# Moving layernorm centring and two time-step operations from VectorE to ScalarE, and folding a router constant into its matmul

## The chip, the cores and the metric

The kernel runs on one core of one Trainium2 chip. The core has a tensor engine (TensorE, PE in the profile) for matmuls and transposes, VectorE (DVE), ScalarE (ACT), GpSimd (POOL) and the queue that issues transfers (SyncE, SP). Each engine carries out its own instructions strictly in order; an instruction that has to wait for another engine holds up all that stands behind it in its queue. The metric is the device time of one execution in microseconds. Three runs of the kernel before took 2607.37, 2610.11 and 2611.04, a median of 2610.11.

## The reference

The input x has 4 sequences of 256 tokens with 512 features, all float32. Four pre-layernorm blocks are applied one after the other:

```
x = x + attention(layernorm(x))      # block 1: gated linear attention, 32 heads of 128
x = x + router(layernorm(x))         # block 2
x = x + state_space(layernorm(x))    # block 3: 128 heads of 64, 8 groups
x = x + adapters(layernorm(x))       # block 4: 64 adapters of rank 16, the 16 best per token

layernorm(x) = (x - mean) / sqrt(var + 1e-5)          # over the 512 features

router(n):   scores  = softmax(n @ Wr.T + b)          # 64 experts
             w       = scores, where among the token's 8 largest, else 0
             out     = n * sum(w) + w @ expert_bias

time steps of blocks 1 and 3:  dt = softplus(n @ Win.T + dt_bias)
```

In block 3 and in block 1 the time steps scale the values and give decays by a cumulative sum along the tokens. Block 4 takes for each token a softmax over its 16 largest router scores and multiplies the 64x16 hidden values by these gates before the second matrix.

## The kernel before, in words

x is held on the chip as 8 tiles k.x[0] to k.x[7] of 128 tokens by 512 features. Tiles 0 to 3 are half 0, tiles 4 to 7 half 1, and each block is run half by half, so that half 1 of one block runs beside half 0 of the next. For the matmuls with weights, the normalized x is turned (features on the partitions) and split into two fp32r parts, xs_hi and xs_lo, and so are the weights: the high part is a cast on ACT (L138), the low part a subtraction on POOL (L141). A projection (proj, L193) is three matmuls for each of four feature chunks. Weights come in 512 KB pieces into a small number of raw buffers (raw_wx, raw_wo, raw_wa, raw_wb and so on); a piece's transfer can start when the piece before it in its buffer has been split.

Layernorm: moments (L82) takes bn_stats (L86) and bn_aggr (L88) on DVE and rstd = (var + eps)^-0.5 on POOL (L90 and L91). centre (L95) makes xn = (x - mean) * rstd in one DVE operation (L99) over 128x512, 32 of them in the kernel. turned (L103) transposes xn in four pieces on PE (L107). In blocks 1, 3 and 4, normalize (L111) then takes xs_hi with ACT (L124) and xs_lo with DVE (L125), and centres a later tile; xn has one buffer there. In block 2 the router's own loop does the same with xT (ACT, L604) and the score matmul (ps_lg, L596).

Time steps: steps_of (L206) projects to ps_dt, adds the bias with DVE into vT (L216), transposes it (L220), copies it to dt with DVE (L221), and goes on with the softplus by DVE and ACT in turn, a cumulative sum on PE and a transfer of the sum (cum), which comes back spread over the partitions (gb). There are four: each half of blocks 1 and 3.

Router: router (L574) has a route generator for each half. After softmax and top 8, the four tiles' weights are transposed (ps_t, L627) and copied by ACT to wT (L629, 64x512). For each tile POOL makes gain = 1 + sum(w)*rstd and a constant sum(w)*rstd*mean (L634 to L636), DVE computes x = x*gain - constant (L638), PE wT by expert_bias (o2, L642), and DVE adds that to x (L643).

State space: state_space (L649) has for each of 8 groups and each half the convolution (conv, L702, ACT L707 and three DVE operations L709), decay matrices m (L748; products with cb on DVE, exponentials on ACT), a mixer (L789: ps_y, xs, yh on ACT L813, yl on DVE L814) and an output matmul (ps_o, L849) that is added up in acc (L853 on ACT, L855 on DVE). At the end of a half x is updated by acc times r (L858), where r is a power on POOL (L835).

Adapters: adapters (L934) projects the normalized x to the router scores (ps_lg), takes the 16 largest (L971 to L991), turns the gates (gT, L996), writes them out and reads them back spread over partitions (gate, L1042), and multiplies the hidden values by them (L1051). wb is the second matrix, split as others by ACT (L1023) and POOL (L1024).

The order of the work is set on two levels. Lists written by hand (STEP1, SIDE1, STEP3, SIDE3) say which piece of a block follows which, and generators of the neighbouring block are pumped in between. On top of this the tile framework schedules with a simulated timeline, TileContext with schedule_with_timeline_sim=True, which fixes the order on every engine's queue when the kernel is built. So an edit of one operation can put many others in another order.

Of the kernel before, what the change touches and what calls it, by code (L numbers as in the profile page):

```python
# [11 lines left out]
F32 = mybir.dt.float32  # L12
# [6 lines left out]
P = 128  # L19
# [62 lines left out]
def moments(k, tc, t, tag):  # L82

    nc = tc.nc
    stats = k.small([P, 6], f"stats_{tag}_{t}", "ln_stats")
    nc.vector.bn_stats(stats, k.x[t])  # L86
    mv = k.small([P, 2], f"mv_{tag}_{t}", "ln_mv", 6)
    nc.vector.bn_aggr(mv, stats)  # L88
    rstd = k.small([P, 1], f"rstd_{tag}_{t}", "ln_rstd", 6)
    nc.gpsimd.tensor_scalar_add(rstd, mv[:, 1:2], EPS)  # L90
    nc.gpsimd.tensor_tensor(rstd, rstd, k.neghalf[:, 0:1], ALU.pow)  # L91
    return mv[:, 0:1], rstd


def centre(k, tc, t, of, tag, into="xn"):  # L95

    bufs = 1 if into == "xn" else 2
    xn = k.wk.tile([P, HID], F32, tag=into, name=f"xn_{tag}_{t}", bufs=bufs)
    tc.nc.vector.tensor_scalar(xn, k.x[t], *of, ALU.subtract, ALU.mult)  # L99
    return xn  # L100


# [103 lines left out]
def steps_of(k, tc, half, w, n, bias, amp, top, dt, start, cum, tag, spare, weigh=False, into="xn"):  # L206

    nc = tc.nc
    ps = proj(k, tc, w, half, f"dt{tag}_{half}", k.bank)
    room = k.wk.tile([P, FREE], F32, tag=into, name=f"room{tag}_{half}", bufs=1 if into == "xn" else 2)
    vT = room[0:n, :]
    nc.vector.tensor_scalar_add(vT, ps[0:n, :], bias)  # L216
    yield
    ps = k.psum.tile([P, HT, n], F32, tag=k.bank, name=f"ps_v{tag}_{half}")
    for t in range(HT):
        nc.tensor.transpose(ps[:, t, :], vT[:, t * P:t * P + P], k.ident[0:n, 0:n])  # L220
    nc.vector.tensor_copy(dt, ps.rearrange("p (b z) h -> p b z h", b=2))  # L221
    yield True


    spare = k.wk.tile([P, FREE], F32, tag=spare, name=f"e{tag}_{half}", bufs=4)
    e = spare[:, 0:HT * n].rearrange("p (b z h) -> p b z h", b=2, z=2)
    u = room[:, 0:HT * n].rearrange("p (b z h) -> p b z h", b=2, z=2)
    d = start.rearrange("p k h b -> p (k h b)")[:, 0:HT * n].rearrange(
        "p (b z h) -> p b z h", b=2, z=2
    )  # L230
    nc.vector.scalar_tensor_tensor(e, dt, -1.0, dt, ALU.mult, ALU.max)
    k.act(e, e, AF.Exp, scale=-1.0)
    nc.vector.tensor_scalar_add(u, e, 1.0)
    yield True
    k.act(d, u, AF.Ln)
    nc.vector.scalar_tensor_tensor(e, u, -1.0, e, ALU.add, ALU.subtract)
    nc.vector.scalar_tensor_tensor(d, u, -1.0, d, ALU.add, ALU.min)
    k.act(u, d, AF.Exp, scale=-1.0)
    nc.vector.scalar_tensor_tensor(dt, dt, 0.0, d, ALU.max, ALU.add)
    nc.vector.tensor_tensor(e, e, u, ALU.mult)  # L240
    nc.vector.tensor_tensor(dt, dt, e, ALU.subtract)
    if top is not None:
        nc.vector.tensor_scalar(dt, dt, 0.0, top, ALU.max, ALU.min)
    al = spare[:, 0:HT * n].rearrange("p (t h) -> p t h", t=HT)
    nc.vector.tensor_tensor(al, dt.rearrange("p b z h -> p (b z) h"), mid(amp, HT), ALU.mult)
    yield
    ps = k.psum.tile([n, HT, P], F32, tag=k.bank, name=f"ps_cum{tag}_{half}")
    for t in range(HT):
        nc.tensor.matmul(ps[:, t, :], al[:, t, :], k.upper, start=True, stop=True)
    cumT = room[0:n, :]  # L250
    nc.scalar.copy(cumT, ps.rearrange("h t l -> h (t l)"))
    for z in range(2):
        nc.sync.dma_start(
            cum[z].rearrange("h (b l) -> h b l", b=2),
            cumT.rearrange("h (b z l) -> h z b l", b=2, z=2)[:, z],
        )
    ps = k.psum.tile([P, 2, 2, n], F32, tag=k.bank, name=f"ps_in{tag}_{half}")
    nc.tensor.matmul(
        ps.rearrange("p b z h -> p (b z h)"), k.upper, spare[:, 0:HT * n],
        start=True, stop=True,  # L260
    )
    within = start[:, 0:2].rearrange("p z h b -> p b z h")
    across = start[:, 2].rearrange("p h b -> p b h")
    nc.vector.tensor_scalar_mul(within, ps, -1.0)
    yield True
    ps = k.psum.tile([P, 2, n], F32, tag=k.bank, name=f"ps_tail{tag}_{half}")
    nc.tensor.matmul(ps, k.lower, al[:, 0::2, :], start=True, stop=True)
    if weigh:

        nc.vector.tensor_scalar_max(e, dt, 1.2e-38)  # L270
        k.act(e, e, AF.Ln)
        nc.vector.tensor_tensor(across, ps, e[:, :, 0, :], ALU.add)
        nc.vector.tensor_tensor(within, within, e, ALU.add)
    else:
        k.act(across, ps, AF.Exp)
        nc.vector.tensor_tensor(across, across, dt[:, :, 0, :], ALU.mult)
    yield
# [296 lines left out]
def router(k, tc, io):  # L574
# [4 lines left out]
    nc.sync.dma_start(wr, io["L0_ffn_router_weight"])  # L579
    bias = k.room[:, 5 * SEQ - NE:5 * SEQ]  # L580
    nc.sync.dma_start(bias, io["L0_ffn_router_bias"].partition_broadcast(P))
    eb = k.room[0:NE, 6 * SEQ:8 * SEQ]
    nc.sync.dma_start(eb, io["L0_ffn_expert_bias"])

    def route(half):

        tiles = [HT * half + at for at in range(HT)]
        of = [moments(k, tc, t, "2") for t in tiles]
        lg = k.small([P, HT, NE], f"lg2_{half}", "lg", 1)
        xn = centre(k, tc, tiles[0], of[0], "2")  # L590
        yield
        for at in range(HT + 1):
            if at:
                ps = k.psum.tile([P, NE], F32, tag=k.bank, name=f"ps_lg2_{tiles[at - 1]}")
                for c in range(KC):
                    nc.tensor.matmul(  # L596
                        ps, xT[:, c, :], wr[:, c, :],
                        start=(c == 0), stop=(c == KC - 1),
                    )
                nc.vector.tensor_tensor(lg[:, at - 1, :], ps, bias, ALU.add)  # L600
            if at < HT:
                tag, bufs = ("y", 4) if half else ("xd", 2)
                xT = k.wk.tile([P, KC, P], F32, tag=tag, name=f"xT_{tiles[at]}", bufs=bufs)
                nc.scalar.copy(xT, turned(k, tc, xn, f"xn_2_{tiles[at]}"))  # L604
            if at + 1 < HT:
                xn = centre(k, tc, tiles[at + 1], of[at + 1], "2")
            yield at == HT
        sm = k.small([P, 2, HT], f"sm2_{half}", "sm")
        nc.vector.reduce_max(sm[:, 0, :], lg, axis=AX.X)
        nc.vector.tensor_tensor(lg, lg, last(sm[:, 0, :], NE), ALU.subtract)  # L610
        k.act(lg, lg, AF.Exp)
        yield
        nc.vector.reduce_sum(sm[:, 0, :], lg, axis=AX.X)
        nc.vector.reciprocal(sm[:, 0, :], sm[:, 0, :])
        nc.vector.tensor_tensor(lg, lg, last(sm[:, 0, :], NE), ALU.mult)

        top = k.small([P, HT, 16], f"top2_{half}", "top", 1)[:, :, 0:8]
        rest = k.small([P, HT, NE], f"rest2_{half}", "rest", 1)
        for at in range(HT):
            nc.vector.max(top[:, at, :], lg[:, at, :])  # L620
            nc.vector.match_replace(rest[:, at, :], top[:, at, :], lg[:, at, :], -1.0)
        nc.vector.scalar_tensor_tensor(lg, rest, 0.0, lg, ALU.is_lt, ALU.mult)
        nc.vector.reduce_sum(sm[:, 1, :], top, axis=AX.X)
        yield
        ps = k.psum.tile([NE, HT, P], F32, tag=k.bank, name=f"ps_t2_{half}")
        for at in range(HT):
            nc.tensor.transpose(ps[:, at, :], lg[:, at, :], k.ident)  # L627
        wT = k.wk.tile([P, HT, P], F32, tag="xd", name=f"wT2_{half}")[0:NE]
        nc.scalar.copy(wT, ps)  # L629
        yield  # L630

        by = k.small([P, 2, HT], f"by2_{half}", "sm")
        for at, (mean, rstd) in enumerate(of):
            nc.gpsimd.tensor_tensor(by[:, 0, at:at + 1], sm[:, 1, at:at + 1], rstd, ALU.mult)  # L634
            nc.gpsimd.tensor_tensor(by[:, 1, at:at + 1], by[:, 0, at:at + 1], mean, ALU.mult)
        nc.gpsimd.tensor_scalar_add(by[:, 0, :], by[:, 0, :], 1.0)  # L636
        for at, t in enumerate(tiles):
            nc.vector.tensor_scalar(  # L638
                k.x[t], k.x[t], by[:, 0, at:at + 1], by[:, 1, at:at + 1], ALU.mult, ALU.subtract
            )  # L640
            ps = k.psum.tile([P, HID], F32, tag=k.bank, name=f"ps_o2_{t}")
            nc.tensor.matmul(ps, wT[:, at, :], eb, start=True, stop=True)  # L642
            nc.vector.tensor_add(k.x[t], k.x[t], ps)  # L643
            yield

    return route
# [596 lines left out]
```

## Time and profile before

| | |
|---|---|
| median of three runs | 2610.11 us |
| the profiled execution's own time | 2612.82 us |
| its span in the profile | 2611.1 us |
| mean granted clock of TensorE in it | 0.978 of full speed |
| DVE centring L99, 32 times | 25.5 us busy, 547 ns median, 2182 ns the longest |
| ACT activations of 128x512 | 583 to 724 ns mean, by their operands |
| DVE L638, 8 times | 5.6 us busy, 541 ns median |

The profile is of one execution. A group of instructions is given by line, engine and operation with its count, its busy time and the mean duration of one. The chain of work that ended last is followed back from the last instruction, at each step to what released it. A time is counted from the start of the span. "xn<-x,mv,rstd" means that xn is written from x, mv and rstd. The granted clock (PEclk) tells at which share of its full speed TensorE was run in a stretch.

In the span, block 1 lasts to about 955 us, with half 0 of blocks 2 and 3 beside its end from about 690; half 1 of block 2 and the first part of block 3 follow until about 1070; block 3 goes on to about 2480, and block 4 stands at the end.

### The profile page before, as it was taken

Reading aid. Unit: us, or ns where it says so; the run is one execution under the profiler, and the core shown is the slowest. Engines: PE = TensorE matmul, PEld = TensorE weight load, DVE = VectorE, ACT = ScalarE, POOL = GpSimd, SP = SyncE. Lnnn points to the kernel's source line nnn. Section 1 sums busy time; section 2 is a strip of 40 time slices with the busy share of each in tenths; the row PEclk is TensorE's granted clock in tenths of the full one; section 3 lists DMA queues with packets and bytes.
Section 4 is the critical chain, followed back from the end, with each engine's and each line's share of the span. In section 5 each row is a group of like instructions: output and inputs, shape, how many; then the busy total and the mean of one; then the engine's idle time right before and its main releaser. Section 6 shows DMA issues by size and latency. Waiting matters only on the chain.

```text
span 2611.1 us, 35577 instructions
## 1 busy us (share of the span) xinstructions
PE 2475.6 (95%) x13488; PEld 2001.8 (77%) x13488; DVE 2082.7 (80%) x2694; ACT 1533.4 (59%) x2109; POOL 1530.1 (59%) x996
## 2 busy tenths in 40 slices
PE   7899999999999888889999999999999999999889
PEld 5677787788777676668878788788787887887667
DVE  5678777778789767688897988888888878879963
ACT  2556556566665555465765665756757657657631
POOL 4445444546565445577674874765756766757840
PEclk9899999999999988999999999999999999999989
DMA  3212111212221222232322222323222222313221
GB/s 105 74 49 65 57 49 56 58 59 87 88 93 57 77 89 69 69 108 86 98 90 65 89 89 68 103 65 89 95 75 89 89 69 88 101 61 104 90 77 67
DMA packets 82891, 206.18 MB, mean 79 GB/s; under 512 B 8672, under 2 KB 10592, under 8 KB 82720
## 3 DMA queue, kind: packets, MB, share of 16 engines
q1 hardware_dynamic: 82720, 203.90, 25.3%
q8 instruction: 107, 1.75, 0.3%
q14 instruction: 64, 0.52, 0.1%
HBM read 200.86 MB, written 3.01 MB: 78 GB/s over the span
## 4 chain that ended last, share of the span: by engine, by line
PE 60%; DVE 24%; ACT 6%; POOL 5%; issue 4%; DMA 2%; SPq 0%; POOLq 0%; ACTq 0%; DVEq 0%
PE ps_g L200 12%; PE ps_o L849 8%; PE ps_x L200 6%; PE ps_o L458 6%; PE ps_q L200 6%; DVE conv L709 5%; DVE m L748 5%; PE ps_y L795 3%; PE ps_y L411 3%; PE ps_sc L399 2%; DVE x L858 2%; PE ps_bc L200 2%; DVE m L293 2%; PE ps_v L200 2%; PE ps_h L200 2%
## 5 line engine op out<-in xcount | busy, mean ns | idle before, releaser
L200 PE MATMUL ps_g<-xs_hi,wg_h 128*128 128x512 f32 x768 | 309.8, 403 | 17.5 <-ACT wg_h L138 7.3
L200 PE MATMUL ps_g<-xs_lo,wg_h 128*128 128x512 f32 x768 | 305.5, 398 | 0.0
L200 PE MATMUL ps_g<-xs_hi,wg_l 128*128 128x512 f32 x768 | 304.1, 397 | 1.2 <-POOL wg_l L141 1.2
L748 DVE TENSOR_TENSOR m<-m,cb 128x1536 f32<-128x1536 f32 x128 | 263.8, 2073 | 47.8 <-ACT m L1110 43.4
L709 DVE SCALAR_TENSOR_TENSOR conv<-ps_x,cw,conv 128x510 f32<-128x510 f32 (+2 forms) x384 | 271.1, 739 | 17.6 <-ACT conv L707 14.4
L1107 ACT ACT_TABLE_LOAD x193 | 247.6, 1283 | 4.0 <-PEq L1231 0.8
L141 POOL TENSOR_TENSOR wo_l<-raw_wo,wo_h 128x1024 fp32r<-128x1024 f32 x60 | 154.6, 2578 | 136.6 <-ACT wo_h L138 136.5
L293 POOL TENSOR_TENSOR m<-gb,start 128x512 f32<-128x512 f32 x128 | 152.9, 1197 | 137.6 <-PE ps_y L795 94.4
L1110 ACT ACTIVATE xs<-conv,cb 128x512 f32<-128x512 f32 x128 | 91.8, 724 | 239.6 <-DVE conv L709 236.6
L809 POOL TENSOR_TENSOR xs<-xs,sg 128x512 f32<-128x512 f32 x128 | 201.2, 1572 | 42.9 <-DVE xs L805 42.3
L849 PE MATMUL ps_o<-wo_h,yh 128*128 128x512 f32 x512 | 213.0, 416 | 9.8 <-DVE acc L855 6.9
L295 POOL TENSOR_SCALAR_AFFINE_SELECT m<-m 128x1024 f32<-128x1024 f32 x160 | 216.7, 1355 | 0.8 <-DVE m L293 0.7
L200 PE MATMUL ps_x<-xs_hi,wx_h 128*128 128x512 f32 x512 | 206.4, 403 | 7.8 <-DVE conv L709 7.8
L849 PE MATMUL ps_o<-wo_h,yl 128*128 128x512 f32 x512 | 201.1, 403 | 6.3 <-DVE yl L814 6.2
L200 PE MATMUL ps_x<-xs_lo,wx_h 128*128 128x512 f32 x512 | 204.9, 400 | 0.0
L200 PE MATMUL ps_x<-xs_hi,wx_l 128*128 128x512 f32 x512 | 203.6, 398 | 0.0
L849 PE MATMUL ps_o<-wo_l,yh 128*128 128x512 f32 x512 | 203.2, 397 | 0.0
L823 POOL TENSOR_TENSOR sqs<-sqs,sq 128x512 f32<-128x512 f32 x112 | 174.7, 1560 | 48.5 <-ACT sq L821 48.1
L141 POOL TENSOR_TENSOR wx_l<-raw_wx,wx_h 128x1024 fp32r<-128x1024 f32 x38 | 97.8, 2575 | 174.4 <-DVE conv L709 118.7
L795 PE MATMUL ps_y<-m,xd 128*64 128x128 f32 x2048 | 178.2, 280 | 14.5 <-DVE m L748 13.8
L141 POOL TENSOR_TENSOR wg_l<-raw_wg,wg_h 128x1024 fp32r<-128x1024 f32 x60 | 159.1, 2652 | 54.8 <-ACT wg_h L138 52.8
L200 PEld LDWEIGHTS ps_g<-xs_hi,wg_h 128*128 128x128 f32 x768 | 144.8, 189 | 60.2 <-issue 14.9
(281 smaller groups left out, 6975.0 us busy)
## 6 DMA issues: line engine op xcount, KB each, us to landing
gb<-cum SPq DMA_DIRECT2D x160, 512.0 KB
raw_wx<-in_L_attn_in_x_dram SPq DMA_DIRECT2D x38, 512.0 KB
raw_wg<-in_L_attn_in_gate_dram SPq DMA_DIRECT2D x38, 512.0 KB
raw_wo<-n_L_attn_out_proj_w_dram SPq DMA_DIRECT2D x38, 512.0 KB
raw_wq<-in_L_attn_Wq_dram SPq DMA_DIRECT2D x22, 512.0 KB
raw_wg<-in_L_attn_Wg_dram SPq DMA_DIRECT2D x22, 512.0 KB
raw_wo<-in_L_attn_Wo_dram SPq DMA_DIRECT2D x22, 512.0 KB
raw_wkv<-in_L_kv_dram SPq DMA_DIRECT2D x11, 512.0 KB
```

Source lines behind the costliest of these rows:

```text
L141: nc.gpsimd.tensor_tensor(lo, w, hi.bitcast(F32), ALU.subtract)
L200: tc.nc.tensor.matmul(ps, a[:, c, :], b[:, c, :], start=(c == 0 and n == 0), stop=(c == KC - 1 and n == 2))
L293: engine.tensor_tensor(m[:, blk], gb[:, min(blk, 1)], last(at, P), ALU.add)
L295: nc.gpsimd.affine_select(out=causal, in_=causal, compare_op=ALU.is_ge, fill=GONE, base=0, pattern=[[0, 8], [1, P]], channel_multiplier=-1,)
L458: nc.tensor.matmul(ps, y[:, 2 * h + b, :], w[:, h, :], start=(i == 0), stop=(i == 5))
L709: nc.vector.scalar_tensor_tensor(acc[:, :, j:], ps[:, :, :SEQ - j], cw[:, ch, TAPS - 1 - j:TAPS - j], acc[:, :, j:], ALU.mult, ALU.add,)
L748: made = nc.vector.tensor_tensor(mh, mh, cbs[p.g, p.half].rearrange("p z b l -> p z (b l)").unsqueeze(2) .to_broadcast([P, 3, 2, 2 * P]), ...
L795: one = nc.tensor.matmul(ps_y[h * D:h * D + D, 2 * b + z, :], p.xe[:, n, b, h, :] if blk == 2 else xd[:, 2 * b + zs, h, :], m[:, blk, 2 * ...
L809: nc.gpsimd.tensor_tensor(xs, xs, p.sg[n], ALU.mult)
L823: nc.gpsimd.tensor_tensor(total, total, sq, ALU.add)
L849: nc.tensor.matmul(ps, y[:, at], w[:, n, :], start=(i == 0), stop=(i == 5))
L1107: load = nc.scalar.preload_act_table_set(table)
```

## The change

Four edits are made together.

1. In blocks 2 to 4 (24 tiles) the centring is an ACT activation, Identity with a scale and a bias per partition: xn = rstd*x + shift. The shift, -mean*rstd, is one more POOL operation on 128x1 after each rstd. Block 1 (tag "1") keeps its DVE operation.
2. In steps_of the bias is added by an ACT activation and dt copied by ACT.
3. In the router the constant per token isn't subtracted by DVE any more. sum(w)*shift is written by POOL as a 65th column of the weights (the tile "wide"), which is transposed with them, and expert_bias gets a 65th row of ones, so that the matmul o2 adds it.
4. x*gain + o2 is one DVE operation, in the place of L638 and L643.

```diff
 def moments(k, tc, t, tag):
...
-    rstd = k.small([P, 1], f"rstd_{tag}_{t}", "ln_rstd", 6)
+    of = k.small([P, 2], f"rstd_{tag}_{t}", "ln_rstd", 6)
+    rstd, shift = of[:, 0:1], of[:, 1:2]
     nc.gpsimd.tensor_scalar_add(rstd, mv[:, 1:2], EPS)
     nc.gpsimd.tensor_tensor(rstd, rstd, k.neghalf[:, 0:1], ALU.pow)
-    return mv[:, 0:1], rstd
+    if tag != "1":
+        nc.gpsimd.tensor_scalar(shift, mv[:, 0:1], rstd, -1.0, ALU.mult, ALU.mult)
+    return mv[:, 0:1], rstd, shift
 
 def centre(k, tc, t, of, tag, into="xn"):
...
-    tc.nc.vector.tensor_scalar(xn, k.x[t], *of, ALU.subtract, ALU.mult)
+    mean, rstd, shift = of
+    if tag == "1":
+        tc.nc.vector.tensor_scalar(xn, k.x[t], mean, rstd, ALU.subtract, ALU.mult)
+    else:
+        tc.nc.scalar.activation(xn, k.x[t], AF.Identity, bias=shift, scale=rstd)
     return xn
...
-    nc.vector.tensor_scalar_add(vT, ps[0:n, :], bias)
+    nc.scalar.activation(vT, ps[0:n, :], AF.Identity, bias=bias)
...
-    nc.vector.tensor_copy(dt, ps.rearrange("p (b z) h -> p b z h", b=2))
+    nc.scalar.copy(dt, ps.rearrange("p (b z) h -> p b z h", b=2))
...
-    eb = k.room[0:NE, 6 * SEQ:8 * SEQ]
-    nc.sync.dma_start(eb, io["L0_ffn_expert_bias"])
+    eb = k.room[0:NE + 1, 6 * SEQ:8 * SEQ]
+    nc.sync.dma_start(eb[0:NE, :], io["L0_ffn_expert_bias"])
+    nc.gpsimd.memset(eb[NE:NE + 1, :], 1.0)
...
-        lg = k.small([P, HT, NE], f"lg2_{half}", "lg", 1)
+        wide = k.small([P, HT, NE + 1], f"lg2_{half}", "lg", 1)
+        lg = wide[:, :, 0:NE]
...
+        nc.vector.reduce_sum(sm[:, 1, :], top, axis=AX.X)
+        by = k.small([P, HT], f"gain2_{half}", "r")
         nc.vector.scalar_tensor_tensor(lg, rest, 0.0, lg, ALU.is_lt, ALU.mult)
-        nc.vector.reduce_sum(sm[:, 1, :], top, axis=AX.X)
+        for at, (_, rstd, shift) in enumerate(of):
+            nc.gpsimd.tensor_tensor(by[:, at:at + 1], sm[:, 1, at:at + 1], rstd, ALU.mult)
+            nc.gpsimd.tensor_tensor(wide[:, at, NE:NE + 1], sm[:, 1, at:at + 1], shift, ALU.mult)
+        nc.gpsimd.tensor_scalar_add(by, by, 1.0)
         yield
-        ps = k.psum.tile([NE, HT, P], F32, tag=k.bank, name=f"ps_t2_{half}")
+        ps = k.psum.tile([NE + 1, HT, P], F32, tag=k.bank, name=f"ps_t2_{half}")
         for at in range(HT):
-            nc.tensor.transpose(ps[:, at, :], lg[:, at, :], k.ident)
-        wT = k.wk.tile([P, HT, P], F32, tag="xd", name=f"wT2_{half}")[0:NE]
+            nc.tensor.transpose(ps[:, at, :], wide[:, at, :], k.ident)
+        wT = k.wk.tile([P, HT, P], F32, tag="xd", name=f"wT2_{half}")[0:NE + 1]
         nc.scalar.copy(wT, ps)
         yield
-        by = k.small([P, 2, HT], f"by2_{half}", "sm")
-        for at, (mean, rstd) in enumerate(of):
-            nc.gpsimd.tensor_tensor(by[:, 0, at:at + 1], sm[:, 1, at:at + 1], rstd, ALU.mult)
-            nc.gpsimd.tensor_tensor(by[:, 1, at:at + 1], by[:, 0, at:at + 1], mean, ALU.mult)
-        nc.gpsimd.tensor_scalar_add(by[:, 0, :], by[:, 0, :], 1.0)
         for at, t in enumerate(tiles):
-            nc.vector.tensor_scalar(
-                k.x[t], k.x[t], by[:, 0, at:at + 1], by[:, 1, at:at + 1], ALU.mult, ALU.subtract
-            )
             ps = k.psum.tile([P, HID], F32, tag=k.bank, name=f"ps_o2_{t}")
             nc.tensor.matmul(ps, wT[:, at, :], eb, start=True, stop=True)
-            nc.vector.tensor_add(k.x[t], k.x[t], ps)
+            nc.vector.scalar_tensor_tensor(
+                k.x[t], k.x[t], by[:, at:at + 1], ps, ALU.mult, ALU.add
+            )
             yield
```

## The prediction

> **What bounds the kernel now.** I read the page's busy shares first, then busy time and granted clock by stretch, then the chain that ended last in the two stretches where TensorE (PE) is not dense, and last the rows of the touched lines.
>
> ```profile
> PE 2475.6 (95%) x13488; PEld 2001.8 (77%) x13488; DVE 2082.7 (80%) x2694; ACT 1533.4 (59%) x2109; POOL 1530.1 (59%) x996
> ```
>
> ```profile
> core 0: us, PE busy (x) PEld busy (x) DVE busy (x) ACT busy (x) POOL busy (x), PEclk, DMA share, GB/s
> ...
> 955.00:1070.00 115.00, 92.75 (x434) 69.93 (x434) 79.01 (x122) 55.00 (x77) 52.96 (x49) 0.81 0.24 76
> ...
> 1240.00:2480.00 1240.00, 1212.94 (x7461) 987.87 (x7460) 1067.30 (x1281) 796.76 (x1091) 833.89 (x524) 1.00 0.28 85
> 2480.00:2545.00 65.00, 56.61 (x254) 44.29 (x253) 42.62 (x93) 22.42 (x37) 28.88 (x29) 0.87 0.24 78
> ```
>
> PE is 95% busy: where it is dense, work taken off VectorE (DVE) is worth nothing. In the dense stretch from 1240 to 2480 nothing changes. The change works in four places: the start, half 0 of blocks 2 and 3 (690 to 905, beside block 1), half 1 of the same blocks (955 to 1070: 22 us of idle PE and a clock of 0.81), and the adapters' start (2480 to 2545, clock 0.87). Half 1's chain:
>
> ```profile
> 954.92 1.73 DVE xn L99
> 956.64 1.96 DVE conv L709 x3
> ...
> 969.93 1.75 DVE m L748
> 971.67 0.47 DVE xn L99
> 972.14 0.04 issue
> 972.18 1.13 PE ps_xn L107 x4
> ...
> 1004.28 0.48 ACT wT L629
> 1004.76 0.04 issue
> 1004.80 3.34 PE ps_o L642 x4
> ```
>
> A centring stretched to 1.73 us stands ahead of the convolutions; the next one, 0.47, stands behind two products m on DVE's in-order queue, and PE waits for it. Then o2 (L642) waits for wT on ScalarE (ACT). The touched line, and ACT's rows nearest to its new price:
>
> ```profile
> L99 DVE TENSOR_SCALAR xn<-x,mv,rstd x32: 516/547/2182, 7.2 to 2525.1; 128x512 f32<-128x512 f32 x32
> ...
> who waited for it (us, times):
>   PEld ps_xn L107: 12.3, 5
>   PE ps_xn L107: 10.9, 4
> ```
>
> ```profile
> L813 ACT ACTIVATE yh<-xs,nw 128x512 fp32r<-128x512 f32 x128 | 91.9, 718 | 52.9 <-POOL xs L809 52.6
> L821 ACT ACTIVATE sq<-xs 128x512 f32<-128x512 f32 x112 | 69.8, 623 | 20.6 <-POOL sqs L823 20.5
> ```
>
> Last the tail, where DVE is today free when xs_lo of tile 3 is wanted, and x (L858) comes 12 us later:
>
> ```profile
> 2499.91 0.69 DVE L125 TENSOR_TENSOR xs_lo<-ps_xn,xs_hi 128x512 fp32r<-128x512 f32 x1 [0.37 <-ACT xs_hi L124]
> 2509.06 0.42 DVE L971 COPY lg<-ps_lgt 128x256 f32<-128x256 f32 x1 [8.45 <-PE ps_lgt L969]
> ...
> 2512.48 2.75 DVE L858 SCALAR_TENSOR_TENSOR x<-acc,r,x 128x512 f32<-128x512 f32 x4
> ```
>
> **The change part by part.** In the program's order of instructions DVE loses 40 (24 centrings, 8 of the time steps, 8 of L638), ACT gains 32, GpSimd (POOL) gains 24 shifts of 128x1 and a memset; table loads stay 193, and SP's queue keeps nearly its order. Transposes with 65 rows and a wT of 65 partitions get no price: PE streams the same columns, and wT's copy (572 ns) runs over the free size; if not, they would grow by a sixty-fourth. L643 becomes an operation with a scalar and PSUM like L709, 739 ns instead of 676, eight times behind o2: +0.06 each, in DVE's slack. The memset of the row of ones (0.53 for L955's larger one) lies before block 2, where POOL is idle four tenths of the time.
>
> *Prices.* A pointer operand costs ACT about 0.1 (718 against 623, the scaled yh against the plain sq), so a centring with two pointers is estimated at 0.82, between 0.72 (second pointer free) and 0.93 (twice). DVE's median was 0.547, but 1.73 to 2.18 in the stretches named here. The shift has the row of L90, 0.20 to 0.57, on POOL; I take 0.22. So alone a centring costs 0.27 + 0.22 = 0.5 more, and 24 of them 12 us if all lay on the path.
> The Trainium skill, "ScalarE: Activation LUTs", section "Rules for kernel authors", says that additions and multiplications belong on VectorE and not on ScalarE. For one operation the rows agree (0.82 against 0.547); by that rule alone the change would lose 24 x 0.27 = 6.5 us and end near 2616.6. The chain above is why I don't follow it: there the price is the place in the queue.
>
> *Start.* L216 (0.73 to 0.75) and L221 (0.29 to 0.69) become ACT operations; ACT's copies of such sizes take 0.58 to 0.59. ACT's vT copy stands ahead of them for 0.6 and the chain runs on to the transfer of cum: +0.3 (bounds −0.5, if ACT's shorter row counts, and +1.2, two waits of 0.6).
>
> *Half 0 of blocks 2 and 3.* PE is dense (200.7 of 215). Removable are its gaps of 0.56, 0.69 and 0.50 behind stretched centrings, 1.75 together; against them ACT's new centrings stand ahead of sq, sh and rms. L638's four operations (0.54 each) have no waiter, since PE is dense there: nothing, or −2.2 if DVE were the bound. −0.7 (bounds −4, all of these, and +2, four exposed 0.5s).
>
> *Half 1.* Step by step, on PE:
> 1. xn_4 goes to ACT's idle 953.9 to 957.7. The convolutions start 1.7 earlier, bc by about 0.75, for wo_h's cast is now between the two bc.
> 2. xn_5 no longer stands behind both m: on ACT it follows xT of tile 4, and its transposes come near 969 instead of 972.18. Later centrings alternate with xT on ACT, 0.82 where DVE had 0.55, so they give back 0.3 each. Net at y (980.87): −3.4.
> 3. The four L638 (2.68 us from 992.58) stood ahead of a convolution and xs; they go. wT, which stood behind a table load (1.28) and three exponentials (to 1004.28), now stands ahead of them. The wait of 1.99 at 1004.80 ends, o2 starts about 999.2: −5.6 in all.
> 4. After that wait 16 matmuls ran at half rate: the eight of o2 took 7.13 us (half 0's ran at 1.05 a pair, 4.2), and the next twelve 4.64 instead of 2.8. Dense, they save up to 2.9 + 1.8. But acc's copies and then the new centring stand in ACT's queue ahead of the transposes at 1016.57, so I let 2.9 of 4.7 through: −8.5.
> 5. Three centrings leave DVE (0.55, 0.86, 1.46) ahead of the m, yl and xs_lo whose waits on PE are 3.86 and 2.22 long: −1.5. Against it room and dt, on ACT, stand behind the casts wo_h and wx_h (1.05 each; wx_h itself waits for PE), where DVE was free: +0.7. The remaining 0.3 is for step 2's give-back in block 3. Sum −9 (bounds −13, all of 4.7 and more of the waits in 5; and −1, if POOL, which stands on the chain from 1082 to 1106, and the wait for raw_wx after it, keep their dates).
>
> The Trainium skill, "TensorE: Matmul & The Clock Gate", section "What's actually happening", puts the cold clock behind an idle window of about 3.4 us. The row has 16 slow matmuls behind 1.99 us, while 2.01 at 2470.66 left none slow; by the page step 4 would not be there, the sum 2.9 higher. The row decides.
>
> *Tail.* POOL is dense from 2483 to 2500.5 and takes four shifts more (+0.9). Shift 2 stands behind wa_l (2.51), so xn_2 waits for about 2497. xn_3, on ACT, stands behind the cast of wb_3, which waits for its transfer (2500.35 today): cast to 2501.8, xn_3 to 2502.5, PE's transposes 2503.2. On DVE xs_lo_3 now stands behind the four x updates (2.75), and these behind r, whose POOL power (1.03) stands behind wb_3l (2.39): 2501.8 + 2.4 + 1.05 + 2.75 + 0.6 = 2508.6, where it was 2500.5. PE has other work for about half: 4 us idle and 1.8 of half-rate matmuls. In return half 1's statistics come 7 us earlier. The gates come only 2.9 later (today 24 of the block's matmuls stand ahead of their transposes); their transfer (5.46) then lands near 2534 for the first gate, 2536 for the next. Behind it today PE stood idle from 2530 to 2535.9 with 2.2 of cold matmuls after; changed, it has work left from the stall to fill part of that. PE reaches the same remaining work +4 (bounds −3, when the stall is only moved work and the cold start goes; +9, when nothing of the stall is filled).
>
> *Sum.* +0.3 − 0.7 − 9 + 4 = −5.4. The profiled execution took 2612.82 (span 2611.1), 2.7 above the runs' median of 2610.11; so it would be 2607.4, and the median 2604.7. Measured apart from no change is 0.2%, 5.2 us.
>
> **The rivals.**
> *Given back (2609 to 2612).* Half 1's gain runs into POOL (126 of 170 us busy from 1070) and the weights' transfers, and only 2 to 4 us arrive, which the tail takes. For it: POOL is on the chain there. Against it: POOL's work follows PE's and starts earlier too.
> *Slower (2616 to 2622).* The wait of xs_lo_3 behind x, r, wb_3l and the transfer of wb_3 costs its full 8.1, and 2 more by a cold clock. It decides once the tail loses over 5 us more than half 1 gains: a tail of +10 with a half 1 of −3 gives 2617. Against it: PE has matmuls of ps_h that need tiles 0 to 2 alone only in part, and the earlier half 1 pays some.
> *Larger gain (2595 to 2600).* Step 4 arrives whole, −13, and the tail's stall is only moved work: −0.4 − 13 + 2 = −11.4, 2598.7.
> *Nothing moves (2608 to 2612).* DVE at 80% isn't the bound and PE is 95% busy. Against it: PE waited 10.9 us for L99 alone.
>
> **How the numbers follow.** Forecast 0.44, larger gain 0.15, given back 0.13, nothing moves 0.04, slower 0.24: this is more than its mechanism alone deserves, since the reordering may add waits that I don't see. The forecast's own range is 2600 to 2609; two thirds of it, 0.28, lie below 2604.9 and 0.16 above. Faster: 0.28 + 0.15 = 0.43. Same: 0.16 + 0.13 + 0.04 = 0.33. Slower: 0.24. The range leaves out the last part of the larger gain (0.08) and of the slower case (0.12): 2595 to 2618.
>
> **What would show it.** Right: PE's wait for xn before 972 ends by 970; no wait at o2 and its eight matmuls under 5 us; xs_lo_3 on DVE directly behind four x updates near 2508, PE idle there; gates landing near 2534. An ACT centring row near 0.82. Wrong: the wait at o2 back behind another ACT instruction, stretches after 1070 longer by what 955 to 1070 loses, or a tail without the new stall.

## The result, and the profile after

The changed kernel is slower: a median of 2617.38 us over six runs (2612.66 to 2619.31) against 2607.47 over six runs of the kernel before (2603.82 to 2611.04), a ratio of 1.0032 with a 95% interval of 1.0021 to 1.0044 (the two medians alone give 1.0038; ratios in brackets below are of this kind). The forecast was 2604.7. The profiled execution has a span of 2616.0, where that of before had 2611.1.

The busy shares, from the page of the changed kernel:

```profile
PE 2478.8 (95%) x13488; PEld 2007.5 (77%) x13488; DVE 2046.4 (78%) x2654; ACT 1553.5 (59%) x2141; POOL 1536.5 (59%) x1021
```

VectorE lost 36 us of work, ScalarE gained 20 and GpSimd 6, in the direction of the edits (part of the 36 are operations that were stretched before and are not now, see below). TensorE's busy share is where it was, so the 36 us say nothing about the time. Busy time and granted clock by stretch, first the changed kernel (the columns are those of the table shown of before), then the one stretch of before that was not shown:

```profile
955.00:1070.00 115.00, 96.91 (x472) 75.58 (x471) 77.48 (x120) 66.89 (x96) 57.78 (x60) 0.85 0.27 83
1070.00:1240.00 170.00, 151.65 (x903) 120.72 (x902) 132.31 (x153) 97.84 (x132) 124.58 (x72) 0.95 0.30 90
1240.00:2480.00 1240.00, 1223.05 (x7516) 997.11 (x7516) 1060.23 (x1288) 799.72 (x1098) 837.32 (x527) 1.00 0.28 85
2480.00:2545.00 65.00, 52.65 (x229) 39.57 (x226) 33.76 (x82) 25.67 (x41) 27.47 (x35) 0.87 0.21 67
```

```profile
1070.00:1240.00 170.00, 158.50 (x958) 126.12 (x957) 142.38 (x161) 100.37 (x138) 125.83 (x73) 0.99 0.30 92
```

Four things stand in these rows. From 955 to 1070 TensorE is busier by 4 us, as forecast. From 1070 to 1240 it is 6.9 us less busy and carries out 55 matmul records fewer: this is where most time is lost. From 1240 to 2480, where nothing was changed, it is 10 us busier. In the tail it loses 4 us.

Such windows have fixed ends while the kernels run ahead of or behind each other. So I also compared the start of the same matmul in two traces (the k-th of its line) and took the median difference over six microseconds at fixed points of the kernel before. The table gives how far TensorE stands behind the profiled execution of before; negative is ahead. The last column counts the last updates of x in the dense stretch that took over 2.9 us, which is explained below.

```
profiled execution                    765    800    905   1055   1245   2440    end   stretched x
before                               0.00   0.00   0.00   0.00   0.00   0.00   0.00   6
  order of before up to 2440 (e2)    1.23   7.28   4.34   1.53   1.38  -3.16  -0.26   4
  order of before, small op (e7)    -0.40   5.45   2.61   2.80   2.82 -10.03 -10.48   0
changed                              0.22   5.76   6.19  -2.51  10.31  -1.63   4.89   0
  order of changed up to 2440 (e1)   0.06   5.69   6.12  -2.43  10.55  -0.87  -0.19   0
block 2 alone (e4)                   0.38   5.69   2.76  -3.45  -3.55 -12.65 -13.22   2
time steps on VectorE (e5)          -0.04   5.52   5.18  -6.14  -3.88 -16.77 -13.88   0
no centring on ScalarE (e6)          1.92   2.02   1.40  -0.96  12.60  -0.41  -0.92   0
```

The changed kernel thus loses 6.0 us from 765 to 905, gains 8.7 to 1055, loses 12.8 to 1245, gains 11.9 in the dense stretch and loses 6.5 in the tail. The two rows of e2 and e7 warn that one profile isn't enough: in the same order of instructions the stretch from 765 to 905 took 3 us more than in the execution that I had read.

### The profile page after: what moved, and what is told of

Its sections match the earlier page's. It is cut to its first block, busy times and chain, and to the rows that moved or that the text cites. A ratio compares the mean times of both kernels' runs of the same rounds, so it can differ in the third digit from the quotient of the medians.

```text
span 2616.0 us, 35601 instructions
## 1 busy us (share of the span) xinstructions
PE 2478.8 (95%) x13488; PEld 2007.5 (77%) x13488; DVE 2046.4 (78%) x2654; ACT 1553.5 (59%) x2141; POOL 1536.5 (59%) x1021
## 4 chain that ended last, share of the span: by engine, by line
PE 68%; DVE 18%; ACT 4%; POOL 4%; DMA 3%; issue 2%; SPq 0%; POOLq 0%; ACTq 0%; DVEq 0%
PE ps_g L207 15%; PE ps_x L207 10%; PE ps_o L858 9%; PE ps_o L465 6%; PE ps_q L207 5%; PE ps_y L804 4%; DVE m L757 3%; PE ps_bc L207 3%; PE ps_y L418 3%; DVE conv L718 3%; PE ps_sc L406 2%; PE ps_o L1081 2%; DVE m L300 2%; DVE yl L823 2%; PE ps_v L207 2%
## 5 line engine op out<-in xcount | busy, mean ns | idle before, releaser
L858 PE MATMUL ps_o<-wo_h,yh 128*128 128x512 f32 x512 | 211.3, 413 | 13.4 <-DVE acc L864 11.2
L858 PE MATMUL ps_o<-wo_h,yl 128*128 128x512 f32 x512 | 199.4, 400 | 8.0 <-DVE yl L823 7.9
L858 PE MATMUL ps_o<-wo_l,yh 128*128 128x512 f32 x512 | 202.0, 394 | 0.0
```

The lines of the kernel that those rows point to most:

```text
L858: nc.tensor.matmul(ps, y[:, at], w[:, n, :], start=(i == 0), stop=(i == 5))
```

## The experiments

Theory after the result: the loss is made of the tail's queue (as forecast) and of something between 1055 and 1245, and the dense stretch owes its gain to a collision between VectorE and GpSimd. Rivals: the centrings' own price on ScalarE (0.82 against 0.55, plus a shift); block 3's lateness alone, handed on to the tail; the scheduler's new order as such.

### Block 4 back on VectorE, and block 4 alone (e1, e2)

In the changed kernel:

```diff
-    if tag != "1":
+    if tag not in ("1", "4"):
         nc.gpsimd.tensor_scalar(shift, mv[:, 0:1], rstd, -1.0, ALU.mult, ALU.mult)
...
-    if tag == "1":
+    if tag in ("1", "4"):
         tc.nc.vector.tensor_scalar(xn, k.x[t], mean, rstd, ALU.subtract, ALU.mult)
```

> The changed kernel with the centring of block 4 back on VectorE; the other edits stay, and all engines keep the changed kernel's order up to about 2450 us. Between the stages of the two profiles TensorE stands 1.6 us ahead of the kernel before at 2450 and 4.9 behind at the end, so the tail seems to cost 6.5. Theory (the tail's loss comes from the centring on ScalarE, through the queue: xs_lo of tile 3 behind four updates of x): 6.5 us less than the changed kernel, near 2611, the 2.6 us wait of TensorE for xs_lo gone. Rival (the tail's loss comes from what arrives there late from block 3): no change, near 2617.

Measured: 2611.16 (ratio to before 1.0000, 0.9990 to 1.0009). That is 6.2 under the changed kernel's median, which comes from another batch; by the two ratios it is 8.3. From 2440 to the end it falls 0.7 behind, the changed kernel 6.5.

In the kernel before, with the shift and the ScalarE centring for block 4 alone:

```diff
+    if tag in ('4',):
+        tc.nc.scalar.activation(xn, k.x[t], AF.Identity, bias=shift, scale=rstd)
+    else:
+        tc.nc.vector.tensor_scalar(xn, k.x[t], mean, rstd, ALU.subtract, ALU.mult)
```

> The kernel before with the centring of block 4 alone on ScalarE; everything up to about 2450 us in the order of before. Theory: the tail's 6.5 us by itself, near 2614; rival (the tail costs only together with the other edits): within 2 us of before.

Measured: 2611.77 (1.0012, 1.0002 to 1.0022); from 2440 to the end +2.9, which is neither the theory's 6.5 nor the rival's nothing. So the tail's loss needs the centring of block 4 on ScalarE and is not lateness handed on, but it is 2.9 alone and 5.8 beside the other edits (6.5 less e1's 0.7). Its chain in the changed kernel:

```profile
2495.51 3.73 DMA raw_wb<-in_L_ffn_B_dram
2499.24 0.02 issue
2499.26 1.05 ACT wb_3h L1032
2500.32 0.07 issue
2500.39 1.50 POOL wb_3l L1033
2501.88 0.81 issue
2502.69 1.04 POOL r L844
2503.73 0.03 issue
2503.75 2.74 DVE x L867 x4
2506.49 0.61 DVE xs_lo L132
2507.10 0.04 issue
2507.14 4.36 PE ps_lg L207 x11
```

This is the queue that the prediction described, link by link. It comes with the changed kernel's order on VectorE, not with the centring alone: in e2, and in e5 below, block 4 is centred on ScalarE too and TensorE has the changed kernel's order there, but VectorE takes xs_lo ahead of the four updates. In e2:

```profile
2500.95 0.69 DVE L132 TENSOR_TENSOR xs_lo<-ps_xn,xs_hi 128x512 fp32r<-128x512 f32 x1 [1.41 <-ACT xs_hi L131]
2501.62 2.74 DVE L865 SCALAR_TENSOR_TENSOR x<-acc,r,x 128x512 f32<-128x512 f32 x4
```

In these two TensorE doesn't wait for xs_lo, and the tail loses 2.9 in both. What all three have and the kernel before has not is a wait of TensorE for a sum on GpSimd (sqs, 2.55, 1.95 and 2.27 in e2, e5 and the changed kernel). So some 2.9 of the 6.5 go with the centring, and the rest goes with VectorE's order, in which the wait for xs_lo is 2.62. In e1 the same place reads:

```profile
2498.93 0.50 PE ps_lg L207
2499.44 0.47 PE ps_h L207 x2
2499.90 2.59 PE ps_lg L207 x11
```

There ps_lg's eleven matmuls start 7.2 us earlier and take 2.59, where after the wait they took 4.36 (granted clock 1.00 in the one, 0.61 in the other).

### A small delay on GpSimd (e3, e7)

From 1240 to 2440 all engines of the two kernels carry out the same instructions in the same order, and still the changed one is 11.9 faster. The update of x at the end of a group's half, VectorE and GpSimd, in the timeline of the kernel before and then of the changed one:

```profile
1416.89 8.12 DVE L858 SCALAR_TENSOR_TENSOR x<-acc,r,x 128x512 f32<-128x512 f32 x4 [3.28 <-POOL r L835]
1422.07 2.40 POOL L141 TENSOR_TENSOR wx_l<-raw_wx,wx_h 128x1024 fp32r<-128x1024 f32 x1 [1.14 <-ACT wx_h L138]
```

```profile
1427.11 5.90 DVE L867 SCALAR_TENSOR_TENSOR x<-acc,r,x 128x512 f32<-128x512 f32 x4 [3.27 <-POOL r L844]
1432.37 2.90 POOL L148 TENSOR_TENSOR wx_l<-raw_wx,wx_h 128x1024 fp32r<-128x1024 f32 x1 [1.24 <-ACT wx_h L145]
```

The four updates took 2.88, 1.77, 0.74 and 2.96 in the one, and 2.88, 1.77, 0.74 and 0.74 in the other. Before, wx_l starts 0.07 us ahead of the third update's end, and the fourth ends 0.55 after wx_l; changed, wx_l starts 0.03 behind that end, the fourth update is not stretched, and wx_l pays 0.5. (The "30 ns" of the expectation below was read off the rounded starts.) So 0.1 us decide over 2.2, in six groups of the profiled execution of before. In the kernel before, for e3:

```diff
+    if name.startswith("wx") and int(name.split("_")[1]) >= 2:
+        nc.gpsimd.tensor_scalar_add(k.late, hi[:, 0, 0:1].bitcast(F32), 0.0)
     nc.gpsimd.tensor_tensor(lo, w, hi.bitcast(F32), ALU.subtract)
```

> The kernel before with one more GpSimd operation of 128x1 ahead of each subtraction wx_l of block 3 from its third group on, about 0.2 us, that reads wx_h; TensorE and VectorE keep their order. Theory (in the dense stretch the kernel before loses 2.2 us in each of six groups because the fourth update of x starts 30 ns after wx_l on GpSimd and is stretched to 2.96 us, and the changed kernel starts it just ahead): the fourth update falls to 0.75 and the kernel gains up to 12 us, near 2596. Rival (the changed kernel's gain there is only that TensorE came late and the other engines stood ahead): nothing gained, or up to 2 us lost by 26 operations.

Measured: 2608.70 (0.9991, 0.9982 to 1.0000). No update over 2.9 us is left, and each group gains 2.2 there, but TensorE waits 1.2 in each group for a yl that stands behind another, delayed wx_l. So for e7 only the one that collides was delayed:

```diff
+    part = name.split("_")
+    if part[0] == "wx" and int(part[1]) >= 2 and part[2] == "2":
+        nc.gpsimd.tensor_scalar_add(k.late, hi[:, 0, 0:1].bitcast(F32), 0.0)
```

> The kernel before with the small GpSimd operation ahead of one wx_l per group alone, the one that meets the fourth update of x (seven of them, from the third group on); all else in the order of before. Theory (a race on a few tens of ns decides in each of six groups whether the update takes 2.96 or 0.75 us): no update over 2.9 us is left and none of the 1.2 to 1.5 us per group is lost that the delay of every wx_l lost by yl; the dense stretch falls by 2.2 for each stretched update of before, of which one execution had 6 and another 4, so 9 to 13 us, near 2598. Rival: the time moves into another wait, at most 3 us gained.

Measured: 2602.34 (0.9967, 0.9954 to 0.9980), with all other instructions in the order of before. This line in the profiled execution of before and then with the delay of one wx_l:

```profile
L858 DVE SCALAR_TENSOR_TENSOR x<-acc,r,x x64: 737/754/2960, 1134.9 to 2514.5; 128x512 f32<-128x512 f32 x64
```

```profile
L862 DVE SCALAR_TENSOR_TENSOR x<-acc,r,x x64: 737/752/2881, 1137.6 to 2504.4; 128x512 f32<-128x512 f32 x64
```

Seven operations of 0.7 us make the kernel 0.33% faster, 8.6 us (6.9 by the medians). At 2.2 for each that is three or four stretched updates in a usual execution of before. In the order of before the profiles had six (before), four (e2) and, with block 2 alone, two (e4): the count changes from execution to execution, and a part of the spread of before, 2603.8 to 2615.0 over all batches, probably comes from it. The profiles of changed, e1, e5, e6 and e9 have none, without an added operation; that TensorE arrives there with another phase is an inference.

The Trainium skill, "SBUF — State Buffer", section "SBUF: two separate sides", says that VectorE, in an operation with two inputs in SBUF, and GpSimd share one pair of ports by an exclusive lock, and that the one that comes second waits for the whole instruction. The rows agree in the main: 2.96 is near to 0.74 and nearly all of a wx_l of 2.40, and all 27 updates of x over 1 us in the profile of before, like the 22 in that of the changed kernel, end 0.54 or 0.55 us after the end of a GpSimd operation.

### Block 2 alone (e4)

In the kernel before, shift and ScalarE centring for the tag "2" alone.

> The kernel before with the centring of block 2 alone on ScalarE. The changed kernel lost 5.5 us at 778 to 790: a product m on VectorE stretched from 1.18 to 2.71 us beside wq_l on GpSimd, the centring on ScalarE ahead of rms, and then half-rate matmuls. Theory: this comes back whole, +4 to +6 by 800 us, the waits at half 1 partly repay it (xn of tile 5 no longer behind two products m: about 3), total +1 to +4. Rival (it is the scheduler's other order from the four edits together): no loss at 778 to 790.

Measured: 2608.08 (0.9991, 0.9979 to 1.0003). Its profiled execution was the fastest of its ten, 2599.63, so its row in the table flatters it. The stretch from 765 to 800 costs 5.3 here, but executions in the order of before cost 0.0, 6.0, 2.9 and 5.9 there (before, e2, e3, e7). Busy time and granted clock of 765 to 805, before, e2, changed and e6:

```profile
765.00:805.00 40.00, 37.98 (x207) 31.44 (x206) 35.77 (x69) 21.86 (x33) 22.04 (x26) 1.00 0.19 60
```

```profile
765.00:805.00 40.00, 36.10 (x175) 30.10 (x174) 34.33 (x63) 18.67 (x26) 18.73 (x25) 0.87 0.18 60
```

```profile
765.00:805.00 40.00, 36.75 (x178) 30.61 (x177) 30.10 (x58) 20.82 (x30) 20.99 (x29) 0.87 0.18 60
```

```profile
765.00:805.00 40.00, 37.98 (x208) 31.55 (x207) 34.06 (x69) 21.87 (x32) 23.28 (x31) 1.00 0.19 60
```

Without centring on ScalarE the clock stays full in some executions (before, e6) and falls to 0.87 in others (e2, e7); in all seven profiled executions with block 2 on ScalarE (changed, e1, e4, e5, e8, e9, e10) the stretch from 765 to 800 costs 5.2 to 5.6. In the five without it the figures are 0.0, 6.0, 2.9, 5.9 and 0.1. So a part of the loss is the change's, but the profile of before was one of the lucky executions, and "6 us" overstates it. The loss is seen on VectorE and TensorE, before (first line), changed and last e2:

```profile
777.56 1.18 DVE L293 TENSOR_TENSOR m<-gb,room 128x512 f32<-128x512 f32 x1 [0.87 <-PE ps_y L411]
```

```profile
777.80 2.71 DVE L300 TENSOR_TENSOR m<-gb,room 128x512 f32<-128x512 f32 x1 [0.88 <-PE ps_y L418]
...
782.01 0.51 PE L443 MATMUL ps_m<-sl,mean 128*128 128x512 f32 x1 [1.49 <-DVE sl L434]
```

```profile
778.79 3.76 DVE L300 TENSOR_TENSOR m<-gb,room 128x512 f32<-128x512 f32 x1 [0.71 <-PE ps_y L418]
```

In the changed kernel xn stands ahead of wq_h's cast on ScalarE, so GpSimd's wq_l begins at 777.59, just ahead of m, and m is stretched as x was above. But the collision is not the change's alone: in all twelve profiles m ends 0.54 or 0.55 after the end of a GpSimd operation, and its length only tells how long it had to wait for that. With block 2 on ScalarE it takes 2.7 in all seven. Without, it takes 1.18, 1.25 and 1.19 in before, e3 and e6, but 3.76 and 3.75 in e2 and e7, where two more operations of GpSimd come between. So the change makes regular what was chance before; five and seven executions are too few to say more.

### The order between 1055 and 1245 (e5, e6)

The instruction orders fall into two classes there. TensorE's order in the kernel before and with block 2 alone is one; the changed kernel has the other. Place by place, 597 of the 1022 matmuls that start there in the kernel before differ (the 337 of the expectation is another way of counting). The changed kernel without the time steps (e5), and the changed kernel without block 2 (built, not timed), are back in the first class; the kernel before with block 3 alone (built, not timed), or with the time steps and the router's column but no centring (e6), is in the second. In the changed kernel, for e5:

```diff
-    nc.scalar.activation(vT, ps[0:n, :], AF.Identity, bias=bias)
+    nc.vector.tensor_scalar_add(vT, ps[0:n, :], bias)
...
-    nc.scalar.copy(dt, ps.rearrange("p (b z) h -> p b z h", b=2))
+    nc.vector.tensor_copy(dt, ps.rearrange("p (b z) h -> p b z h", b=2))
```

> The changed kernel with the two operations of the time steps back on VectorE; all centring and the router's column stay on ScalarE and TensorE. Built so, TensorE's order between 1055 and 1245 is that of the kernel before but for one matmul, where the changed kernel has some 337 matmul entries elsewhere. Theory (the 12.8 us that the changed kernel loses there are the price of that other order, which the planner took for a small shift of time): they go, the total falls by about 12, near 2605. Rival (the centring on ScalarE beside block 3's own ScalarE work costs it): the loss stays, near 2617.

Measured: 2597.42 (0.9945, 0.9928 to 0.9963). From 1055 to 1245 it loses 2.3 instead of 12.8. It ends below the expected 2605 because in its profile the tail loses 2.9 instead of 6.5 and half 1 gains 11.3 instead of 8.7. For e6, in the changed kernel:

```diff
-    if tag != "1":
+    if tag == "2":
         nc.gpsimd.tensor_scalar(shift, mv[:, 0:1], rstd, -1.0, ALU.mult, ALU.mult)
...
-    if tag == "1":
+    if True:
         tc.nc.vector.tensor_scalar(xn, k.x[t], mean, rstd, ALU.subtract, ALU.mult)
```

> The time steps on ScalarE and the router's column as changed, but every centring on VectorE (the shift is made for the router alone). TensorE's order between 1055 and 1245 is that of the changed kernel but for four entries. Theory (order): the 12.8 us are lost here too, without one centring on ScalarE; half 1's gain of 6 to 9 before it is partly missing; the tail loses nothing; near 2612 to 2620. Rival (centring costs it): nothing lost between 1055 and 1245, near 2608.

Measured: 2612.84 (1.0008, 0.9999 to 1.0018). From 1055 to 1245 it loses 13.6, without one centring on ScalarE. The same stretch of e5 and then e6:

```profile
1070.00:1240.00 170.00, 158.67 (x929) 126.21 (x926) 142.63 (x161) 100.76 (x140) 125.52 (x74) 0.98 0.28 90
```

```profile
1070.00:1240.00 170.00, 150.61 (x904) 119.34 (x903) 134.77 (x155) 95.97 (x130) 121.16 (x70) 0.96 0.29 89
```

TensorE's busy time goes with the order, not with the centring: 158.50 and 158.67 in the one, 151.65 and 150.61 in the other. Such a fixed stretch holds fewer matmuls in the slower kernel. Taken over the same 1023 matmuls, before and then changed, it reads:

```profile
1055.00:1245.00 190.00, 174.57 (x1023) 139.05 (x1023) 156.42 (x181) 113.18 (x156) 131.48 (x76) 0.98 0.29 90
```

```profile
1052.49:1255.31 202.82, 180.55 (x1023) 143.72 (x1023) 153.40 (x181) 113.99 (x156) 131.85 (x75) 0.94 0.27 83
```

Of the 12.8 us, 6.8 are longer waits and 6.0 are the same matmuls taking longer, at a granted clock of 0.94 instead of 0.98.

A rival stays open in e5 and e6 themselves: every run with the time steps on ScalarE has the second order and every run without has the first, so the time steps' own price could be the loss. The trace speaks against it. In the changed kernel the last of them, dt of half 1, ends on ScalarE at 1051.94, before the stretch begins; it starts 2.5 ahead of before (1051.35 against 1053.86), just as far ahead as TensorE is at 1055. The changed kernel without block 2, which keeps the time steps on ScalarE in the first order, would have separated the two.

The largest wait in the second order is the one that ends it; the changed kernel's chain there:

```profile
1229.34 0.73 DVE xs L814
1230.07 2.73 DVE m L300
1232.80 1.31 DVE conv L718 x2
1234.11 0.07 DVE r L843
1234.18 2.43 DVE yl L823
1236.62 0.04 issue
1236.66 0.74 PE ps_o L858 x2
```

TensorE waits 4.55 us for a yl that stands last in VectorE's queue, behind convolutions and a stretched m, and is itself stretched to 2.43 (the shortest yl takes 0.73); e6 has the same wait, 4.75, and the order of before does not. Which link of the new order is the costly one was not separated further.

### Parts put together (e8, e9, e10)

e8: the changed kernel with the time steps and block 4 on VectorE, and the small GpSimd operation of e7.

> The changed kernel without the time steps and without block 4 on ScalarE, so with the centring of blocks 2 and 3 and the router's column, and with the small GpSimd operation of the run before. If the three findings add: half 1 gains 6 to 8.7, half 0 loses 0 to 4, nothing is lost between 1055 and 1245 nor in the tail, and no update of x is stretched (9 to 13): near 2592. If centring on ScalarE is what costs between 1055 and 1245: near 2605.

Measured: 2598.12 (0.9950, 0.9936 to 0.9965). e9 is the same without the added operation.

> The centring of blocks 2 and 3 and the router's column as changed; the time steps and block 4 on VectorE; no added operation. It has TensorE's order of before between 1055 and 1245. The stages of the two runs that lie next to it (time steps on VectorE; the same with the small GpSimd operation) give: by 1055 us 5 to 6 ahead of before, 0 to 2 lost until 1245, the dense stretch 11 to 13 better as long as no update of x is stretched, the tail 1 lost instead of 2.9: near 2596 without stretched updates, 2.2 more for each.

Measured: 2595.36 (0.9948, 0.9934 to 0.9961): the lowest median, 14 us under its batch's 2609.60 for before, though by the ratios e5 (0.9945) and e8 (0.9950) are level with it. Its profile has no stretched update, so the added operation of e8 buys nothing in this order. e10: the kernel before with block 2 alone and the added operation.

> The kernel before with block 2's centring alone on ScalarE and the small GpSimd operation ahead of one wx_l per group. If the two findings add (block 2: 3.5 ahead at 1245, with no other loss; no stretched update: 9 to 13), near 2596, 2608.1 less 2.2 for each of the stretched updates that the run with block 2 alone still had, which were 2 in its profile. Rival: the gain of block 2 was the execution's luck at 780 to 800: near 2602, as the delay alone.

Measured: 2598.91 (0.9960, 0.9947 to 0.9972). The gains of block 2 (0.9991) and of the delay (0.9967) come near to adding, though block 2's own share isn't clear of the noise; its profile gained 3.1 from 905 to 1055, e4's 6.2 in the same order.

## Why the prediction was wrong, point by point

**The sum.** Forecast +0.3 − 0.7 − 9 + 4. Measured by TensorE's position, the changed kernel's two executions against the four in the order of before (before, e2, e3, e7, as far as each is comparable): nothing at the start, about +4.1 from 765 to 905 (6.0 and 6.1 against a mean of 2.0), about −7.8 to 1055 (−8.6 against −0.9), +12.9 to 1245, +6.8 in the tail (6.5 against −0.3). That is +16; the ratio says +8.3, so some 8 come back in the dense stretch.

**The step that failed** is the last sentence on half 1: I let the stages behind 1055 follow TensorE, with "keep their dates" as the worst that could happen, 8 us of gain given back. The prediction says that "the reordering may add waits that I don't see", gives it a chance, and prices it at nothing in the sum. It costs 12.9, more than the whole gain: 6.8 of waits and 6.0 of slower matmuls in the profile. e5 and e6 show that it goes with the order and not with the engine that centres; which link of the order costs it stays open. The rival "given back" had the right place but not the size, since it let the gain run dry instead of letting an order lose time of its own.

**A second one:** "In the dense stretch from 1240 to 2480 nothing changes." The instructions don't; the time does, by 2.2 us for each group in which a collision falls the other way. The profile that I read had all six collisions, and L858 with a longest duration of 2.96 beside a median of 0.75 was there to be read.

**Half 0** was forecast at −0.7 with an upper bound of +2. The bound took four exposed waits of 0.5 and left out that a cast moved back by 0.8 us puts wq_l beside m: m stretched by 1.5, and the clock. The other part of the error was the profile of before, which had the best value of its order; in two of the four executions of that order m is stretched too.

**Half 1, right.** Put back by the 6.25 that the changed kernel is late at 950: the transposes of xn_5 at 974.95 are at 968.7 (forecast 969), y at 983.83 is 3.3 ahead (3.4), o2 at 1006.46 is 4.6 ahead (5.6), the transposes of xn_4 of block 3 at 1015.42 are 7.4 ahead (8.5). Centring, o2 and wT in the changed kernel:

```profile
L106 ACT ACTIVATE xn<-x,rstd x24: 799/816/845, 766.0 to 2527.1; 128x512 f32<-128x512 f32 x24
```

```profile
1001.78 0.56 ACT L645 COPY wT<-ps_t 65x512 f32<-65x512 f32 x1
1006.46 1.88 PE L649 MATMUL ps_o<-room,wT 65*128 65x512 f32 x4
...
1010.03 1.98 PE L649 MATMUL ps_o<-room,wT 65*128 65x512 f32 x4 [0.79 <-DVE x L650]
```

The price of 0.82 from two pointers holds at 0.816; o2's eight matmuls take 3.9 instead of 7.1, at the full clock. A wait of 0.79 for VectorE's L650 in the middle of o2 was not forecast. So the granted clock stayed at 1.00 there, where in the kernel before one wait of 1.99 us had been followed by 16 slow matmuls (0.53 from 1004.8 to 1011.9). The prediction's other row, the wait of 2.01 at 2470.66 that "left none slow", says little: only four matmuls followed before the next wait, of 5.44, and the clock from there to 2476 was 0.72.

**The tail, right in kind.** xs_lo of tile 3 came at 2506.41, 2508.0 on the clock of before (forecast 2508.6), the first gate was there at 2532.8, 2534.4 on that clock (2534). It was mis-sized: 5.8 to 6.8 instead of 4. And the queue behind the four updates is a matter of VectorE's order, as e2 and e5 show, where the same centring costs 2.9 without it. TensorE also waited 2.27 us at 2499.67 for a sum on GpSimd (sqs) ahead of ps_m, which now stands ahead of xn_3's transposes; I had not read that line of TensorE's order. (The text ahead of the prediction gives xn one buffer in blocks 1, 3 and 4; only block 3 has one there. No step rested on it.)

**The rule weighed in the text.** That additions and multiplications belong on VectorE, priced at 0.27 for each of 24, gave 2616.6, and 2617.38 was measured. The agreement is chance: e5, with all 24 centrings on ScalarE, is 0.55% faster than before, and e6, without one, has the same loss between 1055 and 1245.

**The rivals.** "Nothing moves" is out: every stage from 765 on moved. "Slower" was right in sign, by luck: its condition, a tail that loses over 5 us more than half 1 gains, was not met (6.8 against 7.8). Its mechanism took part: e1, without block 4 on ScalarE, is level with before, and e5, with it but in the other order, is faster. "Larger gain" did not come true, and its −13 is more than step 4 whole, which by the prediction's own steps adds 1.8 to −9.

## What to carry to other kernels

Where a scheduler writes the queues, compare the two orders stage by stage, and give every stage that is reordered a price and a range of its own; here the order cost 13 us and the edits themselves gained, and building the edits one by one and in part shows which combinations tip the order. Look in the rows for one operation with two durations: a line with a median of 0.75 and a maximum of 2.96 is a collision that a neighbour's 0.1 us can switch on or off, and one 0.7 us operation per group in the right place was worth 8.6 in all. And read more than one execution of the kernel before: a stretch that varies by 6 us in the same order can't carry a verdict of 5.

## What I had not expected of the hardware

An update of x on VectorE takes 0.74 or 2.96 us by whether GpSimd's wx_l begins 0.07 ahead of the preceding update's end or 0.03 behind it; the loser pays the whole rest in the one case, and GpSimd 0.5 in the other. And the granted clock of one stretch of the same instruction order, 765 to 805, was 1.00 in one execution and 0.87 in two others (e2, e7), with up to 6 us between them; in those two a product m on VectorE, behind GpSimd's operations, took 3.76 and 3.75 instead of 1.18.
